# A list scheduler's TensorE durations, its changes of tile form, and the width of its filling matmuls

## The chip, the core and the metric

The kernel runs on one core of one Trainium2 chip. The metric is the device time of one execution in microseconds (us). The median of three runs is 9199.82 us, and the runs lie between 9196.0 and 9213.82 us.

## What is computed

The input is x, float32, 8 images of 56 x 56 positions with 256 channels. Two layers follow each other, cut here to what matters:

```python
# layer 0: group norm, then routed attention of 49 regions (8 x 8 positions each)
q, k, v = split(qkv_w @ gn(x) + qkv_b)
idx = top_k(mean_of_region(q) @ mean_of_region(k), 4)      # 4 regions for each region
attn = (q * scale) @ keys_of(idx)                          # per head: 64 queries x 256 keys
out = softmax(top_k(attn, 32)) @ values_of_those + depthwise_3x3(v)
x = x + out_w @ out + out_b
# layer 1: attention over a window of 7 tokens, then a recurrence over 3136 tokens
t = tokens(x)
t = t + window_attention(layer_norm(t))
for each token of the image:                               # 8 images side by side
    i, g, o = sigmoid(xi + h @ V_i), tanh(xg + h @ V_c), sigmoid(xo + h @ V_o)
    c = h * c + i * g
    h = o * tanh(c)                                        # is added to t
```

The recurrence is a chain: each of its 3136 steps needs the step before it. Everything else is called row work here.

## The kernel before

**Tiles and stages.** An image is cut into 7 rows of 7 regions. One unit is one row of one image, so there are 56 units, taken row by row through all 8 images. For each of its 7 regions, `region` loads the four routed regions' keys and values (`kg`, `vg`), makes scores on TensorE (`sc`), picks the top 32 of 256 keys with four rounds of VectorE's MAX8 (`top`) and MATCH_REPLACE8 (`left`), makes the probabilities on ScalarE (`pe`, `left`), transposes them on TensorE (`pt_av`), copies them out (`pts`) and multiplies by the values (`pt_av` again). The unit ahead gets its queries and its 3 x 3 convolution meanwhile (`queries_and_lepe`, the convolution in `convolve`, matrices `diag`); the unit behind is projected, normalised, put through the window attention and turned into the recurrence's gate terms (`project`, `window_attention`, tensors `x1d`, `t2d`, `xgd`). Nearly all of these matmuls fill a PSUM bank named `mm`.

**The recurrence.** A step is a chain over three engines: 24 small matmuls (`sums_of`, tile `r_sum`, 8 to 24 columns by 64, column strips of 32), ScalarE's tanh (`r_th`), VectorE's transpose (`r_cell<-r_th`), VectorE's scan (`r_c`), ScalarE's tanh (`r_tc`), VectorE's product (`r_hs`); GpSimd then writes one term for the next step's scan (`r_cell<-r_hs,r_half`). Row p's tokens can be stepped through only when all 8 images have had row p's row work. From step 2688 (`APART`), that is for the last row of tokens, the output gate is taken out of the chain.

**What sets the order.** Nothing is issued as it is written. `_Plan` records every operation with an engine, a planned time on the engine (`held`), a planned time to its result (`late`) and a rank. `_Plan.run` then walks through planned time as a list scheduler: each engine takes its first ready operation by rank, and the chain's operations go first. An operation that is not of the chain starts only if its planned end lies before the chain's next planned need of that engine plus an allowance (`SLACK`, 60 ns for TensorE). Where TensorE has nothing that fits and the next known need is more than `FILL` = 220 ns away, a filling matmul is put in (`fill`, tile `spare`, output 32 columns wide, 128 long, read by nobody). The engines' instruction streams are then written in the planned order, and on the chip each engine goes through its own in order, with semaphores between them. The planned times therefore reach the chip only as an order.

**TensorE's durations before** are in `_time`: 160 ns for a transpose, 5/3 ns for each column of output and 50 ns more for a matmul, and 140 ns more to the result. Bundles of matmuls carry their own pair of numbers in `together(held, late)`: 540 and 740 ns for a pair of score tiles, 280 and 480 for each half of the probabilities times values, 350 and 550 for the denominators, 800 and 1000 for a third of a convolution (L = 8), 680 and 855 for the sums of a step. A change of tile form between two operations has no price of its own there.

All recorded operations stand under line L308 in the profile, and the filling matmul under L661.

Of the kernel before, what the change touches and what calls it, by code (L numbers as in the profile page):

```python
# [19 lines left out]
P = 128  # L20
# [35 lines left out]


HOP = 70
FAR = 10**12
FILL = 220  # L60
LONG = 400
CLEAR = 250
SLACK = {"PE": 60, "DVE": 120, "ACT": 60, "POOL": 60, "SP": 1000}
# [40 lines left out]
def _time(engine, name, view, reads, args, kw):  # L104

    n = max([_count(v) for v in [view] + reads])
    if engine == "SP":
        return 650, 2400 + 9 * n // 4
    if engine == "PE":
        held = 160 if name == "transpose" else 5 * _count(view) // 3 + 50  # L110
        return held, held + 140
    if engine == "POOL":
        t = 180 + 15 * n // 7
        return (1050, 1050) if ALU.pow in args else (t, t)
    if engine == "ACT":
        if kw.get("accum_out") is not None:
            t = 5 * n // 7 + 195
            return t + 90, t + 180
        t = n + 10
        if view.buf.banks:  # L120
            return t + 70, t + 120
        if not any(v.buf.banks for v in reads):
            t += 50
        if isinstance(kw.get("bias"), _View):
            return t + 80, t + 170
        return t, t + 90
    held = 25 * n // 24 + 60
    if name == "reciprocal":
        return 20 * n // 3 + 60, 20 * n // 3 + 150
    if name == "transpose":  # L130
        return held + 40, held + 120
    if name == "tensor_tensor_scan":
        return 2 * n + 80, 2 * n + 170
    if name == "match_replace":
        return held + 65, held + 150
    if name == "scalar_tensor_tensor":
        return held + 20, held + 100
    return held, held + 90
# [72 lines left out]
class _Op:  # L211
    __slots__ = (
        "engine", "trace", "held", "late", "rank", "chain", "before", "open", "due", "start",
        "takes", "pair", "made", "closes", "behind",
    )


# [22 lines left out]
class _Plan:  # L240
# [93 lines left out]
    def add(self, engine, traces, reads, writes, held, late):  # L334
        op = _Op()
        op.engine, op.trace, op.held, op.late = engine, traces, held, late
        op.rank, op.chain = self.mode
        op.rank = (op.rank, len(self.ops))
        op.before, op.takes, op.start = {}, [], None
        op.closes, op.behind = False, None  # L340
        op.pair = engine in ("DVE", "POOL") and sum(
            not v.buf.banks and _count(v) > 8 for v in reads
        ) > 1
        self.ops.append(op)
        for views, write in ((reads, False), (writes, True)):
            for v in views:
                self._depend(op, v, write)
                if v.buf.pool is not None:
                    if not v.buf.users:
                        op.takes.append(v.buf)  # L350
                    if not v.buf.users or v.buf.users[-1] is not op:
                        v.buf.users.append(op)
# [19 lines left out]
    def _edge(self, a, b, whole):  # L372

        gap = a.late + HOP if a.engine != b.engine else a.late + 30 if whole else a.held
        a.before[b] = max(gap, a.before.get(b, 0))


    def run(self, tc, fill):
# [52 lines left out]
        filled = tied = 0  # L431
        locked = {"DVE": 0, "POOL": 0}
        since, closed = 0, None
        while len(done) < len(ops) + filled:
            moved = False
            for e in engines:
                if free[e] > now:
                    continue
                while later[e] and later[e][0][0] <= now:
                    _, rank, op = heappop(later[e])  # L440
                    insort(ready[e], (rank, op))
                if not ready[e]:
                    continue
                due = expected(e)
                until = due + (SLACK[e] if e != 'DVE' else max(20, 1.5 * (due - now)))
                for i, (rank, op) in enumerate(ready[e]):
                    if not op.chain and now + op.held > until:
                        continue
                    if op.pair and locked["POOL" if e == "DVE" else "DVE"] > now:
                        continue  # L450
                    if e == "POOL" and op.pair and op.held > LONG and 0 < at < len(chain):
                        if since > 3:
                            continue
                        op.behind = closed
                    if any(b.free and not self._room(b, made, now) for b in op.takes):
                        continue
                    del ready[e][i]
                    op.start = now
                    free[e] = now + op.held
                    if op.pair:  # L460
                        locked[e] = now + op.late
                        heappush(events, locked[e])
                    heappush(events, free[e])
                    heappush(events, now + op.late + HOP)
                    done.append(op)
                    for b in op.takes:
                        if b.free:
                            made.setdefault(id(b.tag), []).append(b)
                    for b, gap in op.before.items():
                        b.due = max(b.due, now + gap)  # L470
                        b.open -= 1
                        if not b.open:
                            opened(b)
                    if op.chain:
                        at += 1
                        since += 1
                        if op.closes:
                            since, closed = 0, op
                    elif e == "POOL" and op.rank[0] == 0:
                        tied += 1  # L480
                    moved = True
                    break
            if not moved and free["PE"] <= now:

                due = min([expected("PE")] + [op[0] for op in later["PE"][:1]])
                if FILL < due - now < FAR // 2:
                    op = _Op()
                    op.trace, op.start = [fill], now
                    filled += 1
                    done.append(op)  # L490
                    free["PE"] = now + FILL
                    heappush(events, free["PE"])
                    moved = True
            if not moved:
                while events and events[0] <= now:
                    heappop(events)
                if not events:
                    raise RuntimeError("the plan has stopped")
                now = heappop(events)
# [30 lines left out]
def _layers(ctx: ExitStack, tc, a, out):  # L530
# [126 lines left out]

    spare = ps_r.tile([P, 512], F32, name="spare")

    def fill():  # L660
        raw.tensor.matmul(  # L661
            spare[:32, :P], ident[:, :32], ident, start=True, stop=True, skip_group_check=True
        )


# [148 lines left out]
    def queries_and_lepe(b, unit, im, row):  # L814
# [81 lines left out]
        def convolve(m):  # L896
            pl = bank()
            for dx in range(3):
                with nc.together(100 * L, 100 * L + 200):
                    for g in range(4):  # L900
                        nc.tensor.matmul(
                            pl[g * HD : (g + 1) * HD, : L * W], diag[:, m, dx, g, :],
                            row["vs"][:, m, g, :L, dx : dx + W],
                            start=(dx == 0), stop=(dx == 2), skip_group_check=True,
                        )
            nc.scalar.activation(
                row["sum"][:, m, :L].rearrange("p r w -> p (r w)"), pl[:, : L * W],
                AF.Identity, bias=cb[:, m : m + 1],
            )
# [12 lines left out]
    def region(qi, unit, im, row):  # L922
# [34 lines left out]
        probs = []  # L957
        for pair in range(groups // 2):
            both = ps_sc.tile([P, 2, 512], F32, name="sc")
            with nc.rank(0.5), nc.together(540, 740):  # L960
                for g2 in range(2):
                    for t in range(2 if whole else 4):
                        g, k = (2 * pair + g2, t) if whole else (t, g2)
# [47 lines left out]
                nc.scalar.copy(pts, pt)  # L1011

        for k in range(2):
            with nc.together(280, 480):
                for jj in range(2):
                    for g in range(4):
                        i, at = (g, k) if whole else (k, g)
# [5 lines left out]
                        )  # L1023
        inv = small.tile([P, 4], F32, name="inv")
        nc.vector.reciprocal(inv[:, :groups], tot[:, :groups])
        with nc.together(350, 550):
            for k in range(1 if whole else 2):
                for g in range(4):
                    i = g if whole else k
# [308 lines left out]
    def recurrence(blk):  # L1338
# [12 lines left out]
        def step(t):  # L1351
# [10 lines left out]
            more = at % 2 == 0 and at + 2 < SHIFTED  # L1362
            if at < APART:
                with nc.rank(0, chain=True):
                    sums_of(bank_of(at)[:, now], h, (0, 1, 2), (680, 855))
                    th = rwork.tile([P, UJ], F32, name="r_th")
                    nc.scalar.activation(th, bank_of(at)[:, now], AF.Tanh)
                    nc.timed(150, 190)
                    nc.vector.transpose(gates, blocks(th))
# [200 lines left out]
```

## Time and profile before

| what | us |
| --- | --- |
| median of three runs | 9199.82 |
| the profiled execution's own time | 9180.4 |
| its span, first to last instruction | 9178.5 |
| TensorE busy in it, filling matmuls included | 8792.1 |
| VectorE busy | 7559.4 |
| ScalarE busy | 5939.4 |
| GpSimd busy | 3221.5 |
| filling matmuls (`spare`), busy, 14904 records | 2072.2 |

An fp32 matmul is recorded twice (two passes), a transpose once, so 48 records are the 24 matmuls of a step's sums, and two records are one filling matmul. A matmul's recorded duration has the way through the array in it; in a stream of matmuls the distance between starts is the cost. Idle time of an engine means little here, since fillings cover TensorE's; what counts is which operation of the chain is late, step by step.

### The profile page before, as it was taken

Reading aid. Unit: us, or ns where it says so; the run is one execution under the profiler, and the core shown is the slowest. Engines: PE = TensorE matmul, PEld = TensorE weight load, DVE = VectorE, ACT = ScalarE, POOL = GpSimd, SP = SyncE. Lnnn points to the kernel's source line nnn. Section 1 sums busy time; section 2 is a strip of 40 time slices with the busy share of each in tenths; the row PEclk is TensorE's granted clock in tenths of the full one; section 3 lists DMA queues with packets and bytes.
Section 4 is the critical chain, followed back from the end, with each engine's and each line's share of the span. In section 5 each row is a group of like instructions: output and inputs, shape, how many; then the busy total and the mean of one; then the engine's idle time right before and its main releaser. Section 6 shows DMA issues by size and latency. Waiting matters only on the chain.

```text
span 9178.5 us, 500794 instructions
## 1 busy us (share of the span) xinstructions
PE 8792.1 (96%) x203918; PEld 6037.0 (66%) x203918; DVE 7559.4 (82%) x32392; ACT 5939.4 (65%) x23551; POOL 3221.5 (35%) x7747
## 2 busy tenths in 40 slices
PE   7999999999999999999999999999999999999999
PEld 4555556666666666666666666666666666688888
DVE  5776799999999899999899999899999999734443
ACT  4665667776666677676676676677766766534444
POOL 1232344444343343343344443434434444311111
PEclk9999999999999999999999999999999999999999
DMA  6545433333332333333333333233333232210000
GB/s 198 155 129 163 111 106 82 93 92 80 93 91 78 91 84 90 89 85 91 88 82 92 91 82 90 78 93 88 83 92 89 80 90 78 60 28 23 23 24 21
DMA packets 1071271, 798.40 MB, mean 87 GB/s; under 512 B 402366, under 2 KB 1001524, under 8 KB 1068964
## 3 DMA queue, kind: packets, MB, share of 16 engines
q1 hardware_dynamic: 1068964, 766.36, 30.8%
q8 instruction: 1604, 26.28, 1.2%
q14 instruction: 703, 5.76, 0.2%
HBM read 527.08 MB, written 238.88 MB: 83 GB/s over the span
## 4 chain that ended last, share of the span: by engine, by line
PE 52%; DVE 25%; ACT 6%; issue 2%; DMA 1%; SPq 0%; POOL 0%; ACTq 0%; DVEq 0%; POOLq 0%
PE r_sum L308 19%; PE mm L308 15%; PE spare L661 12%; DVE left L308 8%; DVE top L308 6%; DVE r_c L308 3%; PE pt_av L308 3%; PE sc L308 3%; DVE r_cell L308 2%; DVE r_hs L308 2%; ACT pe L308 1%; ACT r_th L308 1%; ACT xln L308 1%; DVE st L308 1%; ACT r_sum L308 1%
## 5 line engine op out<-in xcount | busy, mean ns | idle before, releaser
L308 PE MATMUL r_sum<-r_v,r_hs 128*16 128x64 f32 (+2 forms) x150528 | 2758.0, 220 | 160.4 <-DVE r_hs L308 107.1
L308 PEld LDWEIGHTS r_sum<-r_v,r_hs 128*8 128x8 f32 (+2 forms) x150528 | 2224.2, 96 | 907.8 <-DVE r_hs L308 802.6
L308 POOL TENSOR_TENSOR r_cell<-r_hs,r_half 128x16 f32<-128x16 f32 x3136 | 706.7, 225 | 4012.7 <-DVE r_hs L308 3192.8
L661 PE MATMUL spare<-ident 128*32 128x128 f32 x14904 | 2072.2, 276 | 6.2 <-issue 4.5
L308 DVE MATCH_REPLACE8 left<-top,left 128x256 f32<-128x256 f32 x4704 | 1903.3, 408 | 0.0
L308 DVE MAX8 top<-left 128x8 f32<-128x256 f32 x4704 | 1848.2, 413 | 1.8 <-POOL r_cell L308 0.3
L308 ACT ACTIVATE r_th<-r_sum 128x64 f32<-128x64 f32 x3587 | 802.3, 224 | 1559.4 <-PE r_sum L308 1507.1
L661 PEld LDWEIGHTS spare<-ident 128*32 128x32 f32 x14904 | 1474.8, 110 | 309.6 <-issue 263.4
L308 DVE STREAM_TRANSPOSE r_cell<-r_th 128x64 f32<-128x64 f32 x3136 | 812.8, 259 | 882.5 <-ACT r_th L308 842.2
L308 POOL TENSOR_TENSOR pe<-pe,left 128x256 f32<-128x256 f32 x1568 | 1136.2, 729 | 821.5 <-ACT left L308 397.9
L308 ACT ACTIVATE r_tc<-r_c 128x16 f32<-128x16 f32 x3136 | 696.9, 222 | 717.4 <-DVE r_c L308 696.0
L308 DVE TENSOR_TENSOR_SCAN r_c<-r_cell 128x48 f32<-128x48 f32 x3136 | 910.8, 290 | 86.9
L308 ACT ACTIVATE pe<-sc,nmax 128x256 f32<-128x256 f32 x1568 | 710.9, 470 | 185.5 <-DVE left L308 105.3
L308 ACT ACTIVATE left<-left,nmax 128x256 f32<-128x256 f32 x1568 | 773.8, 502 | 13.8 <-DVE left L308 7.8
L308 PE MATMUL pt_av<-ident,pe 128*128 128x128 f32 x3136 | 691.2, 289 | 49.4 <-ACT pts L308 19.4
L308 PE MATMUL mm<-wu,xlT 128*112 128x256 f32 (+3 forms) x1856 | 732.6, 512 | 2.6 <-ACT xlT L308 1.7
L308 DVE MAX8 top<-sc 128x8 f32<-128x256 f32 x1568 | 620.4, 416 | 80.8 <-PE sc L308 80.4
L308 ACT ACTIVATE r_half<-r_c 128x16 f32<-128x16 f32 x3136 | 655.3, 209 | 0.0
L308 DVE SCALAR_TENSOR_TENSOR r_hs<-r_cell,r_tc 128x16 f32<-128x16 f32 x2685 | 545.4, 203 | 124.5 <-ACT r_tc L308 103.4
L308 DVE MATCH_REPLACE8 left<-top,sc 128x256 f32<-128x256 f32 x1568 | 641.2, 412 | 0.7 <-issue 0.6
L308 ACT COPY pts<-pt_av 128x256 f32<-128x256 f32 x1568 | 574.8, 367 | 97.6 <-PE pt_av L308 89.5
L308 PEld LDWEIGHTS pt_av<-ident,pe 128*128 128x128 f32 x3136 | 375.3, 143 | 349.2 <-issue 190.0
(131 smaller groups left out, 12151.6 us busy)
## 6 DMA issues: line engine op xcount, KB each, us to landing
kg<-kd SPq DMA_DIRECT2D x1568, 64.0 KB
vg<-vd SPq DMA_DIRECT2D x1568, 64.0 KB
vshift<-lines SPq DMA_DIRECT2D x336, 232.0 KB
xgd<-gs SPq DMA_DIRECT2D x224, 336.0 KB
r_gin<-xgd SPq DMA_DIRECT2D x1568, 48.0 KB
xchunk<-xt SPq DMA_DIRECT2D x112, 448.0 KB
lines<-v SPq DMA_DIRECT2D x112, 290.0 KB
xn<-xh SPq DMA_DIRECT2D x56, 560.0 KB
```

The costliest lines, as they stand in the source:

```text
L308: made[:] = [method(*[v.real() if isinstance(v, _View) else v for v in args], **{k: v.real() if isinstance(v, _View) else v for k, v in kw ...
L661: raw.tensor.matmul(spare[:32, :P], ident[:, :32], ident, start=True, stop=True, skip_group_check=True)
```

## The change

The scheduler's durations for TensorE are cut to the matmul alone: 110 ns for a transpose, 42/25 ns a column and 4 ns for a matmul, 190 ns more to the result, and lower pairs for the bundles. Each TensorE operation gets a form by the number of rows that it writes (32, 64 or 128), and an operation whose form differs from the one before it starts 94 ns (`SWITCH`) after that one's end. A row operation that is not of form 32 must also leave room for the change back before the chain's need. Fillings become 128 wide behind an operation that is not of form 32 while more than 530 ns are left, and 32 wide otherwise, and a filling that changes form needs 94 ns more of room. `EASE` is zero for every engine. No operation of the kernel's own is added or taken away; what changes is the order in the engines' streams, and the number and width of fillings.

```diff
+SWITCH = 94
-FILL = 220
+FILL = 218
@@ _time
-        held = 160 if name == "transpose" else 5 * _count(view) // 3 + 50
-        return held, held + 140
+        held = 110 if name == "transpose" else 42 * _count(view) // 25 + 4
+        return held, held + 190
@@ _Plan.add
+            rows = writes[0].shape[0]
+            op.form = 32 if rows <= 32 else rows if rows == 64 else P
@@ _Plan.run
+        form, ended = 32, 0
+        def lag_of(form2):
+            return max(0, ended + SWITCH - now) if form2 != form else 0
...
+                    if e == "PE":
+                        lag = lag_of(op.form)
+                        if not op.chain and op.form != 32 and now + lag + op.held + SWITCH > until:
+                            continue
-                    if not op.chain and now + op.held > until:
+                    if not op.chain and now + lag + op.held > until:
                         continue
...
-                    op.start = now
-                    free[e] = now + op.held
+                    op.start = now + lag
+                    free[e] = now + lag + op.held
+                    if e == "PE":
+                        form, ended = op.form, free[e]
...
-                if FILL < due - now < FAR // 2:
+                whole = form != 32 and due - now > 2 * FILL + SWITCH
+                lag = lag_of(P if whole else 32)
+                if FILL + lag < due - now < FAR // 2:
                     op = _Op()
-                    op.trace, op.start = [fill], now
+                    form = P if whole else 32
+                    op.trace, op.start = [lambda n=form: fill(n)], now + lag
...
-    def fill():
+    def fill(n):
         raw.tensor.matmul(
-            spare[:32, :P], ident[:, :32], ident, start=True, stop=True, skip_group_check=True
+            spare[:n, :P], ident[:, :n], ident, start=True, stop=True, skip_group_check=True
         )
@@ bundles: convolve, scores, values, denominators, sums of a step
-                with nc.together(100 * L, 100 * L + 200):
+                with nc.together(94 * L, 94 * L + 190):
-            with nc.rank(0.5), nc.together(540, 740):
+            with nc.rank(0.5), nc.together(497, 690):
-            with nc.together(280, 480):
+            with nc.together(224, 415):
-        with nc.together(350, 550):
+        with nc.together(218, 410):
-                    sums_of(bank_of(at)[:, now], h, (0, 1, 2), (680, 855))
+                    sums_of(bank_of(at)[:, now], h, (0, 1, 2), (671, 855))
```

More of the change, by code (lines that the diff above doesn't have):

```diff
@@ L58 @@
 HOP = 70
+SWITCH = 94
+EASE = {"PE": 0, "ACT": 0, "POOL": 0, "DVE": 0, "SP": 0}
 FAR = 10**12
-FILL = 220
+FILL = 218
 LONG = 400
@@ L213 @@
         "engine", "trace", "held", "late", "rank", "chain", "before", "open", "due", "start",
-        "takes", "pair", "made", "closes", "behind",
+        "takes", "pair", "form", "made", "closes", "behind",
     )
@@ L340, in add @@
         op.closes, op.behind = False, None
+        op.form = None
+        if engine == "PE":
+            rows = writes[0].shape[0]
+            op.form = 32 if rows <= 32 else rows if rows == 64 else P
         op.pair = engine in ("DVE", "POOL") and sum(
@@ L374, in _edge @@
         gap = a.late + HOP if a.engine != b.engine else a.late + 30 if whole else a.held
+        if a.engine != b.engine and not b.chain and b.rank[0] >= 0.5:
+            gap += EASE[b.engine]
         a.before[b] = max(gap, a.before.get(b, 0))
@@ L446, in run @@
                 for i, (rank, op) in enumerate(ready[e]):
-                    if not op.chain and now + op.held > until:
+                    lag = 0
+                    if e == "PE":
[3 more added lines that the diff above has]
+                    if not op.chain and now + lag + op.held > until:
                         continue
@@ L463, in run @@
                     heappush(events, free[e])
-                    heappush(events, now + op.late + HOP)
+                    heappush(events, now + lag + op.late + HOP)
                     done.append(op)
@@ L469, in run @@
                     for b, gap in op.before.items():
-                        b.due = max(b.due, now + gap)
+                        b.due = max(b.due, now + lag + gap)
                         b.open -= 1
@@ L485, in run @@
                 due = min([expected("PE")] + [op[0] for op in later["PE"][:1]])
-                if FILL < due - now < FAR // 2:
+                whole = form != 32 and due - now > 2 * FILL + SWITCH
+                lag = lag_of(P if whole else 32)
+                if FILL + lag < due - now < FAR // 2:
                     op = _Op()
-                    op.trace, op.start = [fill], now
+                    form = P if whole else 32
+                    op.trace, op.start = [lambda n=form: fill(n)], now + lag
                     filled += 1
                     done.append(op)
-                    free["PE"] = now + FILL
+                    free["PE"] = ended = now + lag + FILL
                     heappush(events, free["PE"])
```

## Prediction

> **What bounds the kernel now.** I read the page's busy shares and slices first, then the windows by stage, then the timeline of a step without row work and of steps with it.
>
> ```profile
> PE 8792.1 (96%) x203918; PEld 6037.0 (66%) x203918; DVE 7559.4 (82%) x32392; ACT 5939.4 (65%) x23551; POOL 3221.5 (35%) x7747
> DVE  5776799999999899999899999899999999734443
> PEclk9999999999999999999999999999999999999999
> ```
>
> TensorE's 96% has the fillings in it, so it bounds nothing by itself. VectorE is at 90% or more only while there is row work. The windows (time on PE, PEld, DVE, ACT, POOL, then clock and DMA) show the stages, and the second fence shows the fillings alone:
>
> ```profile
> 0.00:1340.00 1340.00, 1191.84 (x8321) 705.94 (x8322) 975.89 (x3858) 796.82 (x2278) 393.82 (x732) 0.96 0.52 144
> 1340.00:7960.00 6620.00, 6389.55 (x161927) 4281.01 (x161925) 6103.82 (x26276) 4602.54 (x18571) 2668.26 (x6386) 1.00 0.32 87
> 7960.00:8070.00 110.00, 108.52 (x2704) 78.03 (x2703) 46.28 (x192) 50.97 (x222) 31.70 (x79) 1.00 0.18 47
> 8070.00:8222.00 152.00, 152.00 (x4151) 139.67 (x4150) 49.51 (x216) 48.27 (x244) 16.81 (x73) 1.00 0.08 23
> 8222.00:9173.00 951.00, 949.78 (x26822) 832.19 (x26820) 383.28 (x1848) 440.51 (x2239) 110.33 (x476) 1.00 0.08 23
> ```
>
> ```profile
> 1340.00:7960.00 6620.00, 1096.29 (x7408) 703.17 (x7406) 1.00 0.32 87
> ```
>
> Until 1340 there is row work alone. Then 2573 steps run beside row work at 6620/2573 = 2.573 us each; 47 steps beside the last unit's end; 67 steps with no row work at 2.26; and the last 448, with the shorter chain, at 2.12. A step without row work is the chain and nothing else:
>
> ```profile
> 8161.60 0.18 DVE L308 SCALAR_TENSOR_TENSOR r_hs<-r_cell,r_tc 128x16 f32<-128x16 f32 x1 [0.29 <-ACT r_tc L308]
> 8161.83 0.86 PE L308 MATMUL r_sum<-r_v,r_hs 128*8 128x64 f32 x48
> 8162.51 1.69 PE L661 MATMUL spare<-ident 128*32 128x128 f32 x14
> 8162.76 0.22 ACT L308 ACTIVATE r_th<-r_sum 128x64 f32<-128x64 f32 x1 [1.07 <-PE r_sum L308]
> 8163.86 0.17 DVE L308 SCALAR_TENSOR_TENSOR r_hs<-r_cell,r_tc 128x16 f32<-128x16 f32 x1 [0.29 <-ACT r_tc L308]
> ```
>
> From the product's end (8161.78) to the tanh's start it takes 0.98 us. Beside row work the same stretch is longer, in the step below 4005.19 - 4003.83 = 1.36 us:
>
> ```profile
> 4001.36 0.33 PE L308 MATMUL pt_av<-ident,pe 128*128 128x128 f32 x1
> 4001.62 0.86 PE L308 MATMUL r_sum<-r_v,r_hs 128*8 128x64 f32 x48
> 4002.66 1.06 PE L661 MATMUL spare<-ident 128*32 128x128 f32 x8
> 4003.65 0.18 DVE L308 SCALAR_TENSOR_TENSOR r_hs<-r_cell,r_tc 128x16 f32<-128x16 f32 x1
> 4004.04 0.29 PE L308 MATMUL r_sum<-r_v,r_hs 128*8 128x64 f32 x6
> 4005.19 0.23 ACT L308 ACTIVATE r_th<-r_sum 128x64 f32<-128x64 f32 x1 [0.28 <-PE r_sum L308]
> ```
>
> Taking the chain's rows apart over 2450 such steps, the 0.31 us over the quiet step are: 0.10 with TensorE (sums begin late or are drawn out), 0.08 VectorE not ready, 0.07 ScalarE not ready, and 0.07 in VectorE's scan and product themselves (0.30 and 0.20 instead of 0.26 and 0.18).
>
> **The price of a change of form.** Starts in a stream of one form lie 109 ns apart for a 128-column record (8 filling records: 7 x 0.11 and 0.27 for the last make 1.04 of the 1.06 above). From a lone transpose to the sums it is 1.62 - 1.36 = 0.26; over all 585 such places the median is 203 ns, from a transpose to a 32-wide filling 202, from a 256-column record to the sums 309 against 216 within the stream, from a 448-column one 467 against 376. So a change costs 93 ns, and SWITCH = 94 is right.
>
> **Part by part, from the two programs' orders.** Operations are the same; only fillings change in number, 7452 to 7365, 1863 of them now 128 wide. Behind a transpose a 128-wide filling needs no change, and the transposes and wide matmuls show the same 109 and 216 ns in their streams, so I cost the width itself at nothing.
>
> (1) *Row work per step.* VectorE's last MAX8 stood at step 2561 and stands at 2664; counted from the mark where 1344 of its 6280 are done (steps 151 and 150), the same row work is spread over 2514 steps instead of 2410, 4% less a step. If the 0.31 us shrink in proportion, that is 0.012 us a step.
>
> (2) *What TensorE gets between two sums.* By the rows (109 a transpose, 216, 376 and so on, 218 a filling, 93 a change) a step's content came to 1.624 us where the old formulas planned 1.577: 0.047 us more than planned. By the new formulas plan and rows agree, and the content is 1.586. Changes of form fall from 2.41 to 2.26 a step. What lateness follows from an overrun can be read within the trace: steps whose content overran by 0.15 to 0.2 have sums 0.16 late, those that overran by 0 to 0.05 have 0.06, a slope near 0.3 (for the whole step between 0.2 and 0.45, and nothing is left of it in means over 8 steps or more). So the bounds are 0 and 0.047 a step; I take 0.25 of it, 0.012, as the slope is measured on the chip and the full amount would need every late sum to be TensorE's own doing.
>
> Pace: 2.573 - 0.012 - 0.012 = 2.549 us.
>
> (3) *The end of the row work.* This is what the change gives away. Before, the last gate terms were copied at step 2619, 66 steps ahead of the chain's need. In the new order the last unit's regions end at step 2684, and step 2685 has 121 matmuls between two sums, 34 of them fillings, and 45 VectorE operations of row work: the chain has caught up and stands still while that unit is projected, attended and turned into gate terms. By the rows this is 43 us of TensorE. Two round trips through memory are not covered: the issue of x1d to that of x1s took 8 us in the trace (7981.1 to 7989.4), and loads of gate terms some 4 us more. I take 55; the bounds are 43 and the 96 us that the same unit took before beside the chain (7973.8 to 8070.3). Behind it: next late is nothing, the last 448 steps have the same content as before, 951 us.
>
> (4) *The front.* TensorE's content ahead of the first sums, by the same rows, goes from 1052 to 1068 us, with 52 more VectorE operations, of the ninth unit and later. Taken at 17 us; bounds -10 (it runs on idle time) and 30.
>
> Sum against the profiled execution (9180.4 us, span 9178.5): steps before 2688 took from 1340.6 to 8222.3, 6882 us. Now 17 + 2684 x 2.549 + 55 + 3 x 2.26 = 17 + 6842 + 55 + 7 = 6921, which is 39 us more. The median of the runs shown is 19 us over the profiled execution; I add the 39 to the median: 9239 us.
>
> The Trainium skill, "TensorE: Matmul & The Clock Gate", section "Part 1: The HAM clock gate", speaks against the new filling rule and the standstill: TensorE's clock falls to half after an idle window of some 3.4 us. The rows: the clock was 0.96 in the stage where TensorE waits for loads and 1.00 in every later one; by them the standstill costs 43/0.96, 2 us more, and by the page, as an estimate for the case that it is cold throughout, 43 us more. The new rule leaves at most 218 + 94 = 312 ns unfilled in a step instead of 220, far from such a window. No number of the sum uses this.
>
> **Rivals.** The sum's hinge is the pace: (6882 - 17 - 55 - 7)/2684 = 2.535 us is the point at which nothing changes, 0.038 below the present 2.573.
>
> *Row work is packed by VectorE, and the 104 added steps come nearly free (faster).* VectorE was busy 6104 of 6620 us, 92.2%, or 2.372 us a step. The chain's own part is 0.26 + 0.26 + 0.18 = 0.70 by the quiet rows; the rest, 1.67, falls by 4% to 1.605. At the same 92.2% the pace would be 2.305/0.922 = 2.500, which is 2684 x 0.035 = 94 us less than before. For it speaks that engines whose planned ends are true keep their places; against it, that VectorE's idle time comes from waits for tanh, which do not fall with the row work. It decides from 2.535 down. TensorE's share held constant gives (0.64 + 1.586)/(0.64 + 1.624) x 2.573 = 2.530, 13 us less than before.
>
> *The truer durations don't reach the chain at all (slower, more).* TensorE's overrun vanishes in means over blocks of steps, so the pace may stay between 2.56 and 2.573: 69 to 103 us more than before. For it speaks that 0.2 of the 0.31 us are not TensorE's.
>
> *The parts cancel.* A pace between 2.528 and 2.541 gives less than 0.2% (18 us), about what a measurement of this kernel can tell from no change.
>
> **Chances.** My case, pace from 2.535 to 2.56, 0 to 69 us more: 0.42, of which 0.05 lie within 0.2%. Faster by the first rival: 0.44, of which 0.08 lie within 0.2%. The second: 0.14. So faster 0.36, same 0.13, slower 0.51. The range goes from the first rival's 2.500 (9106) to the pace unchanged (9303). The likeliest case's own range is 9200 to 9270.
>
> **What would show it.** Right: 2.55 us a step between the front and step 2660, one gap of 45 to 65 us in the chain before the last 448 steps, these at 2.12 as before, TensorE's sums 0.01 to 0.03 us earlier after the product than the 1.015 us (product's end to the sums' end) they took. Wrong: a pace below 2.535 with VectorE's share at 92% or above (first rival), VectorE's or ScalarE's part of the 0.31 falling by more than 4%, fillings of 128 columns that take more than 109 ns a record or make the sums behind them late, or gaps in the chain other than the one at step 2685.

## The result and the profile after

The changed kernel takes 9228.69 us (median of 9 runs, 9222.88 to 9239.21) against 9199.48 us (9 runs of the kernel before): a ratio of 1.0032, 95% interval [1.0023, 1.0041]. That is 29 us more, between 21 and 38. The profiled execution took 9225.97 us, its span is 9224.2 us, 46 us more than the span before.

The windows of the changed kernel, with the same columns as before (time on PE, PEld, DVE, ACT, POOL, then the clock, the DMA share and GB/s), cut at the places where its stages change:

```profile
0.00:1339.00 1339.00, 1201.83 (x8497) 721.46 (x8498) 1001.06 (x3936) 802.79 (x2310) 401.64 (x745) 0.96 0.52 145
1339.00:8040.00 6701.00, 6431.44 (x163892) 4400.92 (x163895) 6006.61 (x25982) 4573.48 (x18506) 2629.26 (x6350) 1.00 0.32 85
8040.00:8204.00 164.00, 161.07 (x4191) 114.54 (x4179) 129.08 (x567) 101.87 (x427) 60.58 (x148) 1.00 0.24 63
8204.00:8264.00 60.00, 49.17 (x246) 26.93 (x245) 13.76 (x50) 20.41 (x58) 15.14 (x23) 0.94 0.22 56
8264.00:8270.00 6.00, 5.97 (x176) 5.14 (x176) 2.40 (x12) 3.14 (x14) 2.68 (x6) 1.00 0.22 47
8270.00:9219.00 949.00, 947.08 (x26763) 832.05 (x26761) 382.72 (x1846) 439.12 (x2236) 110.02 (x476) 1.00 0.09 23
```

The fourth line is new. For 60 us VectorE is busy 14 us and ScalarE 20, and not one step of the recurrence ends. The stretch without row work that the kernel before had (8070 to 8222) is gone: row work now runs to the last step that can wait for it. The last window is the old one, 949 us.

The timeline of the standstill, VectorE's product at both ends and some of TensorE's and SyncE's lines between (start us, us, engine, what, idle before and its end):

```profile
8203.36 0.40 DVE L310 SCALAR_TENSOR_TENSOR r_hs<-r_cell,r_tc 128x16 f32<-128x16 f32 x1 [0.17 <-ACT r_tc L310]
...
8208.92 0.31 SPq L310 DMA_DIRECT2D x1d<-x  x1
8211.88 0.91 PE L310 MATMUL mm<-ident,xln 112*128 112x112 f32 x4 [2.90 <-ACT xln L310]
8212.09 1.18 SPq L310 DMA_DIRECT2D x1s<-x1d  x3
8214.99 7.62 PE L310 MATMUL mm<-xc,w 128*128 128x451 f32 x16
8244.83 0.63 PE L310 MATMUL mm<-ident,xln 112*128 112x112 f32 x2 [3.11 <-ACT xln L310]
8251.87 3.86 SPq L310 DMA_DIRECT2D xgd<-gs  x2
8255.83 4.28 SPq L310 DMA_DIRECT2D r_gin<-xgd  x8
8263.91 0.17 DVE L310 SCALAR_TENSOR_TENSOR r_hs<-r_tr,r_tc 128x16 f32<-128x16 f32 x1 [0.21 <-ACT r_tc L310]
```

One unit is projected, normalised, attended and turned into gate terms, each stage waiting for the one before it, and the load of the recurrence's next terms (`r_gin`) is issued at 8255.83 and later. From product to product it is 60.3 us, at step 2684, the only gap over 8 us in the chain.

Three rows of the page show the change on the chain's own engines, first before, then after:

```profile
L661 PE MATMUL spare<-ident 128*32 128x128 f32 x14904 | 2072.2, 276 | 6.2 <-issue 4.5
L308 DVE STREAM_TRANSPOSE r_cell<-r_th 128x64 f32<-128x64 f32 x3136 | 812.8, 259 | 882.5 <-ACT r_th L308 842.2
L308 DVE TENSOR_TENSOR_SCAN r_c<-r_cell 128x48 f32<-128x48 f32 x3136 | 910.8, 290 | 86.9
```

```profile
L685 PE MATMUL spare<-ident 128*32 128x128 f32 (+1 forms) x14730 | 2148.5, 278 | 8.4 <-issue 6.8
L310 DVE STREAM_TRANSPOSE r_cell<-r_th 128x64 f32<-128x64 f32 x3136 | 811.3, 259 | 957.3 <-ACT r_th L310 931.1
L310 DVE TENSOR_TENSOR_SCAN r_c<-r_cell 128x48 f32<-128x48 f32 x3136 | 879.8, 281 | 86.4
```

The scan is shorter, 281 ns instead of 290. VectorE has more idle time while it waits for the tanh: it is not packed more tightly than before.

Over the first 2450 steps the pace (us from product to product) fell from 2.574 to 2.561 us. From the product's end to the end of the sums it is 1.003 us instead of 1.015. Over all 2684 steps ahead of the gap the pace fell only from 2.5616 to 2.5575, since the kernel before ran its last hundred or so steps with little or no row work beside them. So the 46 us are: 58 more for the step at the gap (60.3 instead of 2.1), 11 less for the 2684 steps ahead of it, 1 less for the front.

### The profile page after: what moved, and what is told of

It reads as the page before. It is cut to its first block, busy times and chain, and to the rows that moved or that the text cites. A ratio compares the mean times of both kernels' runs of the same rounds, so it can differ in the third digit from the quotient of the medians.

```text
span 9224.2 us, 500398 instructions
## 1 busy us (share of the span) xinstructions
PE 8797.0 (95%) x203744; PEld 6101.2 (66%) x203744; DVE 7536.1 (82%) x32392; ACT 5940.8 (64%) x23551; POOL 3219.9 (35%) x7747
## 4 chain that ended last, share of the span: by engine, by line
PE 47%; DVE 27%; ACT 7%; issue 2%; DMA 2%; POOL 0%; SPq 0%; ACTq 0%; POOLq 0%; DVEq 0%
PE r_sum L310 17%; PE mm L310 14%; PE spare L685 10%; DVE left L310 9%; DVE top L310 7%; DVE r_c L310 4%; PE pt_av L310 3%; DVE r_cell L310 3%; DVE r_hs L310 2%; PE sc L310 2%; ACT pe L310 2%; ACT r_th L310 1%; ACT xln L310 1%; DVE st L310 1%; DVE t L310 1%
## 5 line engine op out<-in xcount | busy, mean ns | idle before, releaser
L310 PE MATMUL r_sum<-r_v,r_hs 128*8 128x64 f32 (+2 forms) x150528 | 2753.6, 220 | 184.8 <-DVE r_hs L310 115.5
L685 PE MATMUL spare<-ident 128*32 128x128 f32 (+1 forms) x14730 | 2148.5, 278 | 8.4 <-issue 6.8
L685 PEld LDWEIGHTS spare<-ident 128*32 128x32 f32 (+1 forms) x14730 | 1563.7, 131 | 268.6 <-issue 153.0
L310 DVE TENSOR_TENSOR_SCAN r_c<-r_cell 128x48 f32<-128x48 f32 x3136 | 879.8, 281 | 86.4
L310 PE MATMUL mm<-wu,xlT 128*112 128x512 f32 (+2 forms) x1856 | 731.0, 512 | 3.7 <-ACT xlT L310 2.6
```

Of the source, the lines that this page charges most:

```text
L310: made[:] = [method(*[v.real() if isinstance(v, _View) else v for v in args], **{k: v.real() if isinstance(v, _View) else v for k, v in kw ...
L685: raw.tensor.matmul(spare[:n, :P], ident[:, :n], ident, start=True, stop=True, skip_group_check=True)
```

## Experiments

The theory: the time is lost because the chain catches up with row work and stands still for 60 us at the last row; the pace itself is a gain of 0.013 us a step over the first 2450, and comes from TensorE's plan being true. The rivals: the loss is in the pace or in the fillings' width; or the durations don't reach the chain.

**The standstill alone.** Gate terms and residuals of the last row are read from the row before, so that the chain has nothing to wait for at its end; once in the changed kernel (e7) and once in the kernel before (e8).

```diff
-                    xg[n][j, :, :, lo : lo + m].rearrange("g b t u -> (g b) t u"),
+                    xg[n - 4 if t >= APART else n][j, :, :, lo : lo + m].rearrange(
+                        "g b t u -> (g b) t u"
+                    ),
...
-                res[: t1 * nb], t2[n][lo : lo + t1].rearrange("t b g -> (t b) g")
+                res[: t1 * nb], t2[m][lo : lo + t1].rearrange("t b g -> (t b) g")
```

(m is n - 4 in the last row.)

> The changed kernel, but the last row's 451 steps read gate terms and residuals of the row before (four blocks of 112 tokens earlier), so that the last 448 tokens of each image are not the reference's. All row work is still done; only the chain no longer waits for the last unit. In the order the 45 VectorE operations between two steps are gone, and the last gate terms are copied at step 2731. Theory (the loss is the standstill): the 60 us gap at step 2684 goes, and the unit's rest slows some 46 steps by 0.1 to 0.4 us each (5 to 18 us), so 9229 - 60 + 5 to 18 = 9174 to 9187 us, faster than the kernel before by 12 to 25 us, the pace up to step 2660 unchanged at 2.56. Rival (the loss lies in the pace, and the standstill only shows where work was left over): no less than 9215 us.

> The kernel before with the same edit as e7 (the last row's steps read gate terms and residuals of the row before; the last 448 tokens of each image are not the reference's). Theory: the chain never waited there, so nothing changes, 9200 us within 10. Rival (reading the older terms is worth something by itself, by earlier loads): faster by 10 us or more, which would have to be taken off what e7 gains.

Measured: e7 9177.83 us, ratio 0.9976 [0.9966, 0.9986] to the kernel before, with no gap over 8 us and the pace at 2.560. e8 9204.16 us, ratio 1.0003 [0.9994, 1.0012]. The edit is worth nothing where the chain doesn't wait. In the changed kernel it takes away 1.0032 - 0.9976 = 0.0056 of 9200, 52 us, and makes of a loss a gain of 0.24%. The standstill is the loss.

The two kernels here and the next two runs also tell how far one execution's pace can be trusted. Profiles with the order of before (before, e2, e8) have a pace of 2.574 to 2.583 us and sums that end 1.015 to 1.022 us after the product; those with the changed order (changed, e1, e7) have 2.560 to 2.567 and 1.003 to 1.010. The two orders are apart in both, but a difference between two single profiles is uncertain by several thousandths of a us.

**The fillings alone.** e2 is the kernel before with the new filling rule; every other operation stands where it stood. As `SWITCH` is 0 in it, a filling is 128 wide while more than 440 ns are left (530 in the changed kernel) and needs no more room for a change of form. e1 is the changed kernel with fillings of 32 columns only, in the same order.

```diff
# e2, the changed kernel with the old durations and with
-SWITCH = 94
+SWITCH = 0
-FILL = 218
+FILL = 220
# e1
-            spare[:n, :P], ident[:, :n], ident, start=True, stop=True, skip_group_check=True
+            spare[:32, :P], ident[:, :32], ident, start=True, stop=True, skip_group_check=True
```

> The kernel before with the new filling rule alone (old durations, no price for a change of form): 1814 of 7452 fillings are 128 wide, every other operation stands where it stood. Theory (width is worth nothing, the loss is the order's): 9200 us within 10. Rival (128-wide fillings are slower, or leave the change back to the sums' own time): slower, by up to 0.03 us a step or 80 us. Other rival (fewer changes of form, 2.41 to 2.38 a step at 93 ns): faster by 0.003 us a step, 8 us.

> The changed kernel with every filling 32 wide; the order is the same, and changes of form go from 2.26 to 2.36 a step. Theory: the added changes lie in time that is filled anyway, so 9229 us within 10. Rival (128-wide fillings carry some of the gain or the loss): 0.1 changes a step at 93 ns in the chain's way would be 25 us slower; if 128-wide fillings are what costs, it is faster by 10 to 30 us.

Measured: e2 9211.47 us, 1.0008 [0.9999, 1.0017]; e1 9224.06 us, 1.0026 [1.0016, 1.0037], with the same gap of 60.3 us at step 2684. e2 is 1.5 us outside the range given, in a set of runs whose kernel before had 9204.41; by the ratio both lie where the order alone would put them. e2's pace, 2.578, lies between those of the old order in before (2.574) and e8 (2.583). The width is worth nothing that can be measured, which settles that part.

**Durations without the count, and with 70 of its 94 ns.** e3 leaves SWITCH at 0 with the pure durations. v4 counts 70 ns. SWITCH also stands in the clause that leaves room for the change back and in the fillings' rule, so both shrink with it.

```diff
# e3
-SWITCH = 94
+SWITCH = 0
# v4
-SWITCH = 94
+SWITCH = 70
```

> The changed kernel with SWITCH = 0: pure durations, changes of form not counted. The order has 2.30 changes a step, 2.39 fillings (1.51 with the count), last gate terms at step 2688 and 31 VectorE operations of row work in one step at 1341 (another standstill). By the rows TensorE's content overruns its plan by 2.30 x 0.093 = 0.21 us a step, where the kernel before had 0.047 and the changed one none. Theory (an overrun reaches the chain with a slope near 0.3): TensorE's lateness 0.15 a step instead of 0.09, pace 2.61, and standstills of some 60 and 40 us at 2685 and 1341: 9229 + 2684 x 0.05 + 40 = 9400 us, within 60. Rival (the overrun reaches the chain in full): pace 2.75, over 9650 us. Other rival (it doesn't reach it at all): pace 2.56, 9270 us or less.

> The changed kernel with a change of form counted at 70 ns instead of 94, nothing else. Last MAX8 at step 2602, last gate terms at 2661, no standstill in the order; 2.28 changes a step, so an overrun of 2.28 x 0.023 = 0.052 us a step, as large as that of the kernel before. Theory: pace 2.565 to 2.58 (the gain in TensorE's lateness is given back), no gap, 9190 to 9210 us, the same as the kernel before. Rival (the order alone decides, not the overrun): pace 2.55 and 9150 to 9170 us.

Measured: e3 9476.36 us, 1.031 [1.0294, 1.0325], 16 us above the range given. v4 9177.6 us, 0.9990 [0.9981, 0.9999], 12 us below its range in time, its ratio at the edge of no change. The kernel before had 9189.61 in this set of runs. The views that separate them, the same groups of the same window (1340 to 7960), first the kernel before, then the changed kernel, then e3; the last numbers are busy us, mean ns and idle us before:

```profile
L308 PE MATMUL r_sum<-r_v,r_hs 128*8 128x64 f32 (+2 forms) x123504 | 2274.3, 220 | 158.2 <-DVE r_hs L308 105.6 <-issue 27.5
L308 DVE STREAM_TRANSPOSE r_cell<-r_th 128x64 f32<-128x64 f32 x2572 | 663.9, 258 | 306.4 <-ACT r_th L308 266.4 <-POOL pe L308 2.1 <-POOL v L308 1.8
```

```profile
L310 PE MATMUL r_sum<-r_v,r_hs 128*24 128x64 f32 (+2 forms) x124108 | 2279.8, 220 | 180.3 <-DVE r_hs L310 112.7 <-issue 44.4 <-DVE top L310 0.6
L310 DVE STREAM_TRANSPOSE r_cell<-r_th 128x64 f32<-128x64 f32 x2585 | 666.5, 258 | 448.2 <-ACT r_th L310 422.5 <-POOL pe L310 1.6 <-POOL r_cell L310 1.3
```

```profile
L310 PE MATMUL r_sum<-r_v,r_hs 128*8 128x64 f32 (+2 forms) x118508 | 2281.9, 220 | 79.9 <-DVE r_hs L310 34.9 <-issue 28.0
L310 DVE STREAM_TRANSPOSE r_cell<-r_th 128x64 f32<-128x64 f32 x2468 | 644.6, 261 | 559.1 <-ACT r_th L310 516.7 <-POOL nmax L310 1.0
```

In e3 TensorE seldom waits for the product (35 us instead of 113): when the product is done TensorE is still at row work that the plan thought done, the sums begin 0.196 us after the product instead of 0.106, and VectorE stands idle before its transpose. The sums end 1.131 us after the product, 0.128 later than in the changed kernel, and the pace is 2.681, 0.120 more. v4, with 0.052 us of overrun a step, has 1.021 and 2.570, so 0.018 and 0.009 more; the kernel before, with 0.047, had 0.012 and 0.013 more. An overrun reaches the sums with a quarter to a third of its size while it is small and with 0.6 at 0.21 us. The room in the clause is the smaller part: without the clause altogether (e4, next) the sums end 0.005 later. So the earlier sums are the true plan's: 24 ns off in the price of a change make them as late as before. The pace is given back in part, as v4's 2.570 lies between the two orders' ranges.

My expectation for e3 missed twice, and the total comes near its range by luck: the pace was to be 2.61, and the two standstills of some 60 and 40 us did not come. Step 2684 took 2.4 us, and the longest, at 1340, 12.4 us.

**The clause that leaves room for the change back (e4).**

```diff
-                        if not op.chain and op.form != 32 and now + lag + op.held + SWITCH > until:
-                            continue
```

> The changed kernel without the clause that a row operation not of form 32 must leave 94 ns for the change back. In the order the chain runs ahead all the same: last gate terms at step 2689, 22 VectorE operations of row work in one step at 893 and at 1341. Theory: the clause keeps sums from being late (0.01 to 0.03 us a step more without it, pace 2.57 to 2.59) and is not what makes the chain catch up; with standstills at two rows' ends and at the last of some 10 to 30 us each, 9220 to 9290 us, no faster than the changed kernel. Rival (the clause holds row work back and so causes the standstill): 9160 to 9200 us.

Measured: 9183.8 us, 0.9992 [0.9983, 1.0001], against 9194.09 of the kernel before: my expectation missed, and the rival's range holds it. The pace is 2.564, within the range of the changed order, and the gap at the end is 4.6 us. The waits at two rows' ends that the order shows are there, but cost 8.3 and 9.0 us and not 10 to 30: the chain waits there for loads of gate terms (`r_gin`) while VectorE goes on with the next row's MAX8 and MATCH_REPLACE8. So the clause is a part of what holds row work back until the end. It is worth little to the sums: without it they begin 0.121 us after the product instead of 0.106, but end at 1.008 instead of 1.003.

**Giving the row work a little of the chain's time.** Three versions of the changed kernel allow row work to run on further past the chain's need, on ScalarE (v1), on VectorE (v2) or on both (v6); b2 is v2's edit in the kernel before.

```diff
# v1 and v6
-SLACK = {"PE": 60, "DVE": 120, "ACT": 60, "POOL": 60, "SP": 1000}
+SLACK = {"PE": 60, "DVE": 120, "ACT": 100, "POOL": 60, "SP": 1000}
# v2, v6 and b2
-                until = due + (SLACK[e] if e != 'DVE' else max(20, 1.5 * (due - now)))
+                until = due + (SLACK[e] if e != 'DVE' else max(60, 1.5 * (due - now)))
```

> The changed kernel with ScalarE's allowance in SLACK 100 ns instead of 60, nothing else. In the order the last MAX8 stands at step 2641 (before 2561, changed 2664), the last gate terms at 2687, and no step holds more than 9 VectorE operations of row work: the chain does not run out. Theory (the changed kernel loses by its standstill alone, and its pace is a gain of 0.013 a step over before): pace 2.56 to 2.57 and no gap over 15 us, 9229 - 60 + 10 to 25 = 9180 to 9195 us, 5 to 25 us faster than the kernel before. Rival (row work given to ScalarE later in the chain's time costs what the standstill saves): 9215 us or more.

> The changed kernel with VectorE's least allowance 60 ns instead of 20, nothing else. Last MAX8 at step 2628, last gate terms at 2691, no step with more than 9 VectorE operations of row work; 2.23 changes of form a step. Theory: no standstill; VectorE, the engine at 92%, is given work in gaps that the old bound left, 0.02 to 0.04 us late each, so the pace lies between 2.55 and 2.57: 9165 to 9200 us, 5 to 35 us faster than the kernel before. Rival (a late transpose or product goes straight into the chain, 0.04 us a step): pace 2.60, 9260 us or more.

> The changed kernel with both allowances, VectorE's least 60 ns and ScalarE's 100 ns. Last MAX8 at step 2625, last gate terms at 2690, no step with more than 9 VectorE operations of row work. Theory (what counts is that the chain doesn't run out; v2 has reached that): pace 2.545 to 2.56, no gap, 9140 to 9165 us, the same as v2 within 0.2%. Rival (the two gains add): 9110 to 9130 us.

> The kernel before with VectorE's least allowance 60 ns instead of 20 (the edit that gained in v2). In the order it moves almost nothing there: last MAX8 at step 2561 and last gate terms at 2619 as before, 8 fillings more. Theory (v2's gain comes from the true TensorE durations once the chain does not run out; the allowance only keeps it from running out): 9200 us within 12, the same as before. Rival (the allowance is worth 0.5% by itself): 9145 to 9165 us.

| kernel | pace, first 2450 steps | product's end to sums' end | last MAX8 at step (trace) | gap at step 2684 | median us | ratio to before |
| --- | --- | --- | --- | --- | --- | --- |
| before | 2.574 | 1.015 | 2565 | none | 9199.48 | 1 |
| changed | 2.561 | 1.003 | 2667 | 60.3 | 9228.69 | 1.0032 [1.0023, 1.0041] |
| v1 | 2.554 | 0.995 | 2645 | 17.2 | 9158.59 | 0.9966 [0.9954, 0.9978] |
| v2 | 2.550 | 0.988 | 2631 | 5.8 | 9144.97 | 0.9950 [0.9936, 0.9963] |
| v6 | 2.555 | 0.993 | 2628 | 16.7 | 9166.67 | 0.9971 [0.9962, 0.9980] |
| b2 | 2.580 | 1.020 | 2565 | none | 9197.55 | 1.0004 [0.9995, 1.0013] |

The steps of the last MAX8 are counted in VectorE's stream of the trace; the expectations' numbers are three or four lower. The kernel before had 9189.61 us beside v1 and v2, and 9194.09 beside v6 and b2. v1 and v2 beat both kernels; v2's 9144.97 is 20 us below its range. v2's windows show it: the stage between front and last row is 6838 us, against 6882 before.

```profile
0.00:1338.00 1338.00, 1199.76 (x8510) 719.74 (x8514) 1001.56 (x3938) 803.79 (x2314) 402.74 (x746) 0.96 0.52 145
1338.00:8176.00 6838.00, 6600.62 (x168249) 4511.52 (x168241) 6158.85 (x26604) 4700.27 (x18994) 2716.79 (x6518) 1.00 0.32 85
8176.00:9128.00 952.00, 949.86 (x26806) 832.03 (x26804) 384.13 (x1851) 442.57 (x2246) 115.23 (x483) 1.00 0.09 23
```

In the kernel before the allowance alone is worth nothing (b2). Its order hardly moves there, so b2 does not show what the allowance would be worth where it does move it. v1 came out 21 us below its range, and with a gap of 17.2 us that I had thought gone: few VectorE operations in one step of the order do not mean that the chain has its terms. The two gains do not add: v6 is no faster than either, 2 us over its range, and has v1's gap. Why the pace of v1 and v2 is 0.007 and 0.011 below the changed kernel's is not settled, and 0.007 is no more than two executions of one order differ by. The sums end 0.008 and 0.015 earlier, though TensorE's own plan is no truer there than in the changed kernel.

## Why the prediction was right, point by point

The direction, the cause and the size held: 9239 was forecast and 9228.69 came out, inside the likeliest case's own range. In the profile the change is +46 us where the sum had +39. That the two are so close owes something to luck: the front came out 18 us below its term and the pace 22 us above. The terms are these.

**The standstill** (forecast 55, bounds 43 and 96): 60.3 us, 58 more than a step. The 43 us of TensorE's rows became 49 busy ones. The round trip from x1d to x1s was covered better than thought (3.2 us from issue to issue, not 8), and two waits that the sum did not have came in: 2.9 and 3.1 us in which TensorE waits for the normalised tiles, which wait for VectorE and GpSimd. The loads of gate terms, taken at 4 us, took 9.2 from the issue of xgd's store to the copy of `r_gin` (8251.87 to 8261.07), beside the unit's last matmuls. e7 shows that the gap is real time and not moved work.

**TensorE's overrun** (forecast 0.012 us a step, bounds 0 and 0.047): the stretch from product to sums fell by 0.012 (0.014 in the mean of three profiles of each order), and v4 and e3 show that it is the overrun that does it. The slope read within the trace of before was right for an overrun of this size, and the means over blocks, in which nothing was left of it, misled; they were rightly given little weight.

**Less row work a step** (forecast 0.012): this term was mis-sized, and the idea that the parts shrink in proportion did not hold. In proportion, 4% of each part is 0.003. Instead the wait from the scan to the second tanh fell by 0.012 and the scan by 0.011, while the transpose began 0.019 later after its tanh and the product took 0.003 longer, so that 0.001 to 0.002 remained of it. In the stretch between tanh and transpose VectorE is mostly still at a MAX8 or MATCH_REPLACE8: these account for 0.094 of its 0.108 us (0.075 of 0.090 before). A likely reading is that with the sums done earlier the tanh comes earlier, and a VectorE operation that is already running does not end earlier, so that what TensorE gains is in part waited out one engine on. In v4, whose sums are late again, the stretch is 0.093; no run tests it alone, and why the scan and the wait behind it fell by so much is open. The missing 0.010 would be 27 us; the pace over all 2684 steps came to 2.5575 instead of 2.549, 22 us more.

**The front** (forecast +17, bounds -10 and 30): -1 us; the added work ran on idle time. The first product ends between 1333 and 1350 us in the six profiles of the two orders, so single profiles do not tell a few us here.

**The last 448 steps** (nothing): 951 us both.

**The rivals.** VectorE as the engine that packs (pace 2.500) did not come: VectorE's share fell from 92.2% to 89.6% (6007 of 6701 us), and it waited longer for the tanh. That the durations do not reach the chain is refuted by e3 and v4.

**The clock.** Over the 60 us the granted clock was 0.94. It fell to half twice, for 3.41 us each, 2.3 us behind the first of the two waits above and as the second ended:

```profile
8214.14:8217.55 3.41, 3.41 (x8) 1.54 (x8) 0.00 (x0) 0.35 (x2) 0.00 (x0) 0.50 0.26 89
8244.86:8248.27 3.41, 3.41 (x7) 1.51 (x8) 0.00 (x0) 1.25 (x3) 0.00 (x0) 0.50 0.00 0
```

So TensorE was not slow throughout, and the price is at most half of 6.8 us, 3.4 us. The Trainium skill, "TensorE: Matmul & The Clock Gate", section "Part 1: The HAM clock gate", gives an idle window of some 3.4 us as the condition for the half clock. The waits here were shorter, 2.9 and 3.1 us, and the clock fell all the same; the measurement decides.

**The signs that were named.** Of those for being right, the one gap, the last 448 steps and the earlier sums came as said, and the pace up to step 2660 was 2.559 instead of 2.55. Two of those for being wrong came as well: fillings of 128 columns took 112 ns a record and not 109, which costs nothing that can be measured (e1, e2), and ScalarE's part of the 0.31 us fell by far more than 4%, by 0.012 of some 0.07, which VectorE's later transposes took back.

## What to carry to other kernels

Where a planner gives a chain and the work that feeds it to the same engines, making it more exact on one engine also moves the balance between the two: look in the order for the step at which the feeding work ends, against the step that needs it, before looking at the pace. A chain that has a lead to use up looks like a gain until the lead is gone; here 0.013 us a step were won over the first 2450 steps, 11 us over all, and 58 us lost at one place. Without the wait the durations were worth 0.24% (e7); with the lead restored by one allowance, durations and allowance together were worth 0.5% (v2), and how they share it is open.

## What the runs showed of the hardware that was not expected

A filling of 128 columns costs 112 ns a record in its stream against 109 with 32, and begins 109 ns after a transpose where a 32-wide one begins 202 ns after it; in time that is filled anyway neither is seen (e1, e2). TensorE's granted clock fell to half for 3.41 us behind idle times of 2.9 and 3.1 us. An overrun of TensorE's plan does not pass to the chain in proportion: a quarter to a third of 0.05 us (before, v4), but 0.6 of 0.21 us (e3). That e3's overrun has used up the time in which TensorE waited for the product fits its row (35 us of such waits instead of 113) and is not shown further.
